# Layer 0 scan of a two-layer MetaFormer: two PSUM buffers for the product, one for the spread B, two for the front's tiles

## The chip, the cores and the metric

The kernel runs on one core of a Trainium2 chip. The time is the device time of that core in microseconds (us), from a few runs of the same program; a profiled execution of its own gives the trace and the profile page.

## What is computed

The input x is 2 images of 96 channels and 96 x 96 pixels. Layer 0 adds a selective-scan mixer and a small feed-forward network, layer 1 an attention mixer and another such network. The change concerns the scan of layer 0, which the reference states so (cut to the scan):

```python
def step(hst, inputs):
    ut, dt, bt, ct = inputs
    dA = jnp.exp(dt[..., None] * A)
    hst = hst * dA + (dt * ut)[..., None] * bt[:, :, None, :]
    y = jnp.einsum('bkdn,bkn->bkd', hst, ct)
    return (hst, y)
...
out_y = selective_scan(xs4, delta, A, Bs, Cs, Ds.reshape(KG, d_inner))
inv_y = out_y[:, 2:4, :, ::-1]
...
y = out_y[:, 0] + inv_y[:, 0] + wh_y + invwh_y
```

There are 192 inner channels, 16 states per channel and 4 directions (along rows and along columns, each forwards and backwards). The recurrence runs over windows of 6 x 6 pixels, each a sequence of 36 steps of its own. What leads to it (a layer norm, a projection, a 3 x 3 convolution, an offset sampling, and the projections to delta, B and C) and what follows (a layer norm, a gate, a projection, the feed-forward network) are the front and the back below.

## The kernel before

**Stripes.** Layer 0 is cut into 32 stripes: 2 images of 16 stripes, each of 6 rows or 576 tokens. For each stripe there is a front (`_l0_front`), a scan (`_l0_scan`) and a back (`_l0_back`). While stripe n is scanned, the front of stripe n + 1 and the back of an earlier stripe run in between on the same engines.

**Units.** The scan of a stripe is 64 units: 2 halves of the channels (h), 4 directions (o for rows or columns, kk for forwards or backwards), 4 groups of states (i) and 2 halves of the tokens (c). A unit holds 32 channels x 4 states on the 128 partitions, and 3 blocks of channels x 288 tokens along the free axis, 864 elements in all. With 32 stripes that makes 2048 units. A unit u is worked through in this order (`unit` in `_l0_section`):

- TensorE (PE) spreads B of the tokens over the partitions, with a matmul against a 0/1 matrix, into the PSUM tile `B` (L1040)
- VectorE (DVE) multiplies it with delta times u, `dur`, into the PSUM tile `bp` (the product, L1045; 864 floats, so two of PSUM's eight banks)
- VectorE scans: h = h x dA + bp along the tokens, into the SBUF tile `h` (L1060). The decays `dA` come from ScalarE (ACT, L1025), three instructions for two units
- GpSimd (POOL) multiplies h with C, `cre`, in place (L1065)
- PE folds the 4 states of a channel into one by matmuls that add into the PSUM tile `y` (L1077). One `y` tile gathers 32 units; it starts with a matmul of the inputs (L966, L968), and ACT copies it out at the end (L976, L978)

SyncE (SP) issues all loads: `dlr`, `dur` and `cre`.

**The front and the back** hold some matmuls for each stripe (72 steps of the convolution among them, L551), copies and activations out of PSUM on ACT, and elementwise work on POOL (L609 to L615, L743 to L746, L921). VectorE has three small kinds of instruction from there: `xn` (L508), `fxq` (L827) and `Y` (L912). The PSUM tiles of the front and back are all called `p`: one bank each, `P.np` of them in turn.

**The order.** Every operation goes into a plan (`_Plan`) with its engine, a cost, a due time and the tiles that it uses. The planner sets them in order engine by engine: what can start first goes first, and of those what is due first; a tile takes a buffer when one is free. The result is a fixed order on each engine, which the program keeps. At run time each instruction waits, by semaphores, for what it depends on, and an engine stands still behind an instruction that waits. A change in the number of buffers thus changes both the waits and the whole order.

**PSUM in layer 0** before the change: `B` two banks (two buffers), `bp` two banks (one buffer), `y` one, `p` three: all eight. `h` has six buffers (`P.nh`), `dA` two (`P.nda`).

**The hand-set waits.** Besides the dependencies that follow from the tiles, `product` of an even unit (c = 0) is made to wait for what the scan of this unit and of the next will need: the decays of unit u, B of unit u + 1, and the POOL and PE instructions that free the h buffer of unit u + 1. `wait` does this with the list of `P.issued`.

Of the kernel before, what the change touches and what calls it, by code (L numbers as in the profile page):

```python
# [55 lines left out]
def _in_order(k, tc, start, engines=ENGINES):  # L56

    last = {}
    for i in k.nc.cur_bb.bb.instructions[start:]:
        if i.engine in engines:  # L60
            if i.engine in last:
                tc.add_manual_dep(
                    i,
                    last[i.engine].name,
                    mybir.DependencyInfo(
                        mybir.DependencyClass.NoSync, mybir.DependencyReason.DATA
                    ),
                    reason="in_order",
                )
            last[i.engine] = i  # L70
# [915 lines left out]
def _tail(py, b):  # L986

    n = T - HEAD
    return py.ap[NBL * CB :, b * n : b * n + n]


def _l0_section(k, P, S, f, first, o, h, kk, py, at, tau):


    nc = k.nc
    latest = lambda: nc.cur_bb.bb.instructions[-1]

    def wait(keys):
        for other in map(P.issued.get, keys):
            if other is not None:  # L1000
                P.tc.add_manual_dep(
                    latest(), other.name,
                    mybir.DependencyInfo(mybir.DependencyClass.Sync, mybir.DependencyReason.DATA),
                    reason="with_the_product")

    kg = o + 2 * kk
    reps = []
    for name, d in (("dlr", f.dl[kg]), ("dur", f.du[kg])):
        t = S.tile(P.rep, [128, NBL, T], name, 2)
        S.op("sp", 2.6, lambda t=t, d=d: nc.sync.dma_start(  # L1010
            t.ap.rearrange("p b t -> p (b t)"),
            d.ap[:, 3 * h : 3 * h + 3, :].rearrange("c b t -> c (b t)").unsqueeze(1)
            .to_broadcast([CB, NQ, NBL * T])), (d,), (t,), due=at - 9 * tau)
        reps.append(t)
    dlr, dur = reps

    def quarter(i):
        t0, u = at + 2 * i * tau, first + 16 * o + 8 * kk + 2 * i
        cre, dA = S.tile(P.rep, [128, T], "cre", 4), S.tile(P.rep, [128, 2, NBL, H2], "dA", P.nda)
        S.op("sp", 1.0, lambda: nc.sync.dma_start(  # L1020
            cre.ap, f.cd[o].ap[kk, :, i, :].unsqueeze(0).to_broadcast([CB, NQ, T])),
            (f.cd[o],), (cre,), due=t0 - P.early["sp"] * tau)
        for blk in range(NBL):
            def decay(blk=blk):
                nc.scalar.activation(  # L1025
                    dA.ap[:, :, blk, :], dlr.ap[:, blk, :].rearrange("p (c n) -> p c n", c=2),
                    AF.Exp, scale=k.A[:, i, kg, h, blk : blk + 1])
                P.issued["act", u] = latest()

            S.op("act", 0.76, decay, (dlr,), ((dA, blk),), due=t0 - P.early["act"] * tau, tab="e")  # L1030
        for c in range(2):
            unit(u + c, i, c, cre, dA, t0 + c * tau)

    def unit(u, i, c, cre, dA, t0):
        toks = slice(c * H2, (c + 1) * H2)
        pB, bp = S.tile(P.ps, [128, 512], "B", 2), S.tile(P.ps, [128, 1024], "bp", 1)
        ht = S.tile(P.rep, [128, NBL, H2], "h", P.nh)

        def spread():
            nc.tensor.matmul(  # L1040
                pB.ap[:, :H2], k.selb[:, kk, i, :], f.bc[o].ap[:, toks], start=True, stop=True)
            P.issued["B", u] = latest()

        def product():
            nc.vector.tensor_tensor(  # L1045
                bp.ap[:, : NBL * H2].rearrange("p (b n) -> p b n", b=NBL), dur.ap[:, :, toks],
                pB.ap[:, :H2].unsqueeze(1).to_broadcast([128, NBL, H2]), ALU.mult)
            if c == 0:
                free = u + 1 - P.nh
                wait([("act", u), ("B", u + 1), ("pool", free), ("pe", free)])  # L1050

        S.op("pe", 0.3, spread, (f.bc[o],), (pB,), due=t0 - P.early["pe"] * tau)
        S.op("dve", 1.13, product, (dur, pB), (bp,), due=t0 - P.early["dve"] * tau)

        def scan():
            hv, dv = (v.rearrange("p b n -> p (b n)") for v in (ht.ap, dA.ap[:, c]))
            bv = bp.ap[:, : NBL * H2]
            if kk:
                hv, dv, bv = hv[:, ::-1], dv[:, ::-1], bv[:, ::-1]
            nc.vector.tensor_tensor_scan(hv, dv, bv, 0.0, ALU.mult, ALU.add)  # L1060

        S.op("dve", 2.0, scan, (dA, bp), (ht,), due=t0 + (1.35 - P.early["dve"]) * tau)

        def times_c():
            nc.gpsimd.tensor_tensor(  # L1065
                ht.ap, ht.ap, cre.ap[:, toks].unsqueeze(1).to_broadcast([128, NBL, H2]), ALU.mult)
            P.issued["pool", u] = latest()

        S.op("pool", 2.06, times_c, (cre,), (ht,), due=t0 + (2.3 - P.early["pool"]) * tau)

        def states():
            end = o == 1 and kk == 1 and i == NQ - 1

            def part(dst, v, stop):
                if o:
                    v = v.rearrange("p (w j i) -> p w i j", i=WIN, j=WIN)
                nc.tensor.matmul(dst, k.fold, v, start=False, stop=stop)  # L1077

            for blk in range(NBL):
                dst = py.ap[CB * blk : CB * blk + CB]  # L1080
                n = HEAD - H2 if c else H2
                part(dst[:, c * H2 : c * H2 + n], ht.ap[:, blk, :n], end and c == 1)
            if c:
                for blk in range(NBL):
                    part(_tail(py, blk), ht.ap[:, blk, n:], end and blk == NBL - 1)
            P.issued["pe", u] = latest()

        S.op("pe", 1.0, states, (ht,), (py,), due=t0 + (3.5 - P.early["pe"]) * tau)

    for i in range(NQ):  # L1090
        quarter(i)


def _layer0(k, tc, a, x, x2d):


    nc = k.nc
    with ExitStack() as st:
        P = Ctx()
        pool = lambda name, bufs, **kw: st.enter_context(tc.tile_pool(name=name, bufs=bufs, **kw))  # L1100
        cp = pool("l0c", 1)
        P.dram = pool("scr", 1, space=DRAM)
        with ExitStack() as ws:
            tmp = ws.enter_context(tc.tile_pool(name="l0t", bufs=1))
            wps = ws.enter_context(tc.tile_pool(name="l0p", bufs=1, space=PSUM))
            _l0_weights(k, a, cp, tmp, wps, P.dram)
            ffn = _ffn_weights(k, cp, tmp, "f0", a["W1_0"], a["b1_0"], a["W2_0"], a["b2_0"])
        P.rep, P.hand, P.back, P.front = (pool(n, 1) for n in ("rep", "hand", "back", "front"))
        P.ps = pool("ps0", 1, space=PSUM)
        P.tc, P.issued = tc, {}  # L1110
        P.early = {"pe": 60, "act": 60, "dve": -30, "pool": 0, "sp": 8}
        P.np, P.ng, P.nda, P.nh = 3, 5, 2, 6
        start = len(nc.cur_bb.bb.instructions)
        S, tau = _Plan(k), 3.4
        stripes = [(b, s) for b in range(NB) for s in range(NW)]
        F = [Ctx() for _ in stripes]

        def front(n):
            if n < len(stripes):
                t0, t1 = (64 * n - 90) * tau, (64 * n - 12) * tau  # L1120
                _l0_front(k, P, S, F[n], x, *stripes[n], lambda v: t0 + v * (t1 - t0))

        def back(n):
            b, s = stripes[n]
            t0, t1 = (64 * n + 68) * tau, (64 * n + 135) * tau
            _l0_back(k, P, S, F[n], ffn, x[b, :, s * WIN : (s + 1) * WIN, :],
                     x2d[b, :, s * T : (s + 1) * T], lambda v: t0 + v * (t1 - t0))

        front(0)
        for t, name in zip(k.kvq, ("k_w", "v_w", "q_w")):  # L1130

            S.op("sp", 0.2, lambda t=t, name=name: nc.sync.dma_start(t, a[name]), due=64 * tau)
        for n in range(len(stripes)):
            front(n + 1)
            _l0_scan(k, P, S, n, F[n], tau)
            back(n)
        S.issue()
        _in_order(k, tc, start, ENGINES + (mybir.EngineType.SP,))
# [709 lines left out]
def tile_metaformer(ctx: ExitStack, tc: tile.TileContext, a, out):  # L1848
# [34 lines left out]
    scratch = ctx.enter_context(tc.tile_pool(name="x2d", bufs=1, space=DRAM))  # L1883
    x2d = scratch.tile([NB, C, NTOK], F32, tag="x2d", name="x2d")
    _layer0(k, tc, a, a["x"], x2d)
    _layer1(k, tc, a, x2d, out)

# [61 lines left out]
```

## Time and profile before

| | |
|---|---|
| median of 3 runs | 8775.34 us (8774.3 to 8780.41) |
| span of the profiled execution | 8782.9 us |
| busy over the span: VectorE (DVE) | 8004.4 us, 91% |
| TensorE matmuls (PE) | 7366.0 us, 84% |
| ScalarE (ACT) | 6381.2 us, 73% |
| GpSimd (POOL) | 6026.5 us, 69% |
| first and last product (L1045) start at | 146.8 and 6727.2 us |
| mean granted TensorE clock | 0.891 of full speed |

For the profiled execution only the span is known; its run time is not listed apart. The page gives busy shares over the whole span, but layer 1 begins after 6735 us and has other limits, so shares for the change have to be read over the stretch of layer 0. In a row of groups, the first number is the sum of the busy time, the second the mean of one instruction; after the second bar stands the idle time of the engine just before such instructions, and what ended most of it. Start times and durations in a timeline are rounded to 0.01 us. A gap is a start minus the end of the instruction before it on the engine; a negative gap means that the two records overlap.

### The profile page before, as it was taken

How to read it: one execution, taken by the hardware profiler on the slowest of the kernel's cores; microseconds unless marked ns; L12 is line 12 of the kernel's file. 1: busy time of each engine (PE TensorE's matmuls, PEld its weight loads, DVE VectorE, ACT ScalarE, POOL GpSimd, SP SyncE). 2: the span in 40 equal slices, each digit the busy share in tenths (PEclk: the TensorE clock that was granted, in tenths of full speed). 3: DMA queues.
4: the chain of work that ended last, by engine and by line, in shares of the span. 5: the costliest groups of instructions: out<-in, count | busy, mean ns of one | idle time of the engine just before them, and what ended most of it. 6: DMA issues, size and time to landing. Idle time of an engine off the chain costs nothing. (4 is left out here: it accounts for less than half of the span.)

```text
span 8782.9 us, 119686 instructions
## 1 busy us (share of the span) xinstructions
PE 7366.0 (84%) x43653; PEld 3436.2 (39%) x43653; DVE 8004.4 (91%) x5398; ACT 6381.2 (73%) x10720; POOL 6026.5 (69%) x3835
## 2 busy tenths in 40 slices
PE   7888888888888888888888888888865999989998
PEld 4333434434434343343343434334422323542245
DVE  3899999999999999999999999999997898959988
ACT  5677777777777777777777777777764787678867
POOL 4999998988899899898998888898885000010001
PEclk8898888998988888898888889888866999989999
DMA  2444444444444444444444444444442000110001
GB/s 85 139 149 144 145 145 141 146 143 141 142 141 145 137 151 144 142 142 146 145 142 143 142 143 138 145 139 142 142 140 87 19 2 9 34 51 2 3 21 32
DMA packets 339996, 985.64 MB, mean 112 GB/s; under 512 B 50152, under 2 KB 51872, under 8 KB 339104
## 3 DMA queue, kind: packets, MB, share of 16 engines
q1 hardware_dynamic: 337488, 977.74, 35.4%
q8 instruction: 346, 5.67, 0.3%
q14 instruction: 258, 2.11, 0.1%
q10 hardware_dynamic: 1904, 0.12, 0.0%
HBM read 797.19 MB, written 139.25 MB: 107 GB/s over the span
## 5 line engine op out<-in xcount | busy, mean ns | idle before, releaser
L1065 POOL TENSOR_TENSOR h<-h,cre 128x864 f32<-128x864 f32 x2048 | 4124.1, 2023 | 692.6 <-DVE h L1060 493.1
L1060 DVE TENSOR_TENSOR_SCAN h<-dA,bp 128x864 f32<-128x864 f32 x2048 | 3999.8, 1953 | 84.7 <-PE y L1077 6.3
L1025 ACT ACTIVATE dA<-dlr,A 128x576 f32<-128x576 f32 x3072 | 2156.4, 765 | 1098.8 <-DVE h L1060 1015.1
L1045 DVE TENSOR_TENSOR bp<-dur,B 128x864 f32<-128x864 f32 x2048 | 2172.9, 1061 | 295.9 <-PE B L1040 48.7
L1077 PE MATMUL y<-h,fold 128*32 128x288 f32 (+2 forms) x18432 | 1870.7, 452 | 161.6 <-POOL h L1065 152.0
L1040 PE MATMUL B<-bt,selb 128*128 128x288 bf16 x2048 | 642.4, 315 | 963.5 <-DVE bp L1045 951.1
L551 PE MATMUL pc<-xin,off 96*96 96x288 f32 x4608 | 1321.4, 414 | 0.5 <-ACT xin L516 0.4
L1077 PEld LDWEIGHTS y<-h,fold 128*32 128x32 f32 x18432 | 764.3, 119 | 1138.1 <-issue 548.9
L1413 ACT ACTIVATE pr<-sc 128x960 f32<-128x960 f32 (+1 forms) x1080 | 954.1, 937 | 200.3 <-PE sc L1409 180.3
L1493 DVE TENSOR_TENSOR sums<-sums,pr 128x3840 f32<-128x3840 f32 (+1 forms) x240 | 959.1, 3996 | 55.2 <-ACT pr L1413 33.2
L551 PEld LDWEIGHTS pc<-xin,off 96*96 96x96 f32 x4608 | 708.3, 165 | 514.3 <-issue 268.4
L1585 POOL MEMSET vch<- 96x32 f32 x16 | 2.4, 153 | 1296.6 <-DVE dist L1447 1209.3
L1040 PEld LDWEIGHTS <-selb 128*128 128x128 bf16 x2048 | 200.6, 99 | 1303.7 <-DVE bp L1045 797.9
L1409 PE MATMUL sc<-qH,kH 32*128 32x480 f32 (+1 forms) x3240 | 627.2, 602 | 9.7 <-issue 4.9
L1409 PE MATMUL sc<-q,kH 32*128 32x480 f32 (+1 forms) x1080 | 564.5, 602 | 0.0
L1475 PE MATMUL av<-pr,vT 128*32 128x480 f32 (+1 forms) x4320 | 532.6, 564 | 3.7 <-ACT av L1500 3.5
L1666 DVE SCALAR_TENSOR_TENSOR acc<-vch,lepe_w,acc 96x1152 f32<-96x1152 f32 x320 | 469.2, 1466 | 7.9
L867 POOL TENSOR_TENSOR x<-x,fy 96x576 f32<-96x576 f32 x32 | 56.1, 1755 | 480.6 <-ACT fy L866 400.6
L1409 PEld LDWEIGHTS sc<-qH,kH 32*128 32x128 f32 x3240 | 219.2, 184 | 418.3 <-issue 218.4
L724 PE MATMUL pt<-xd,w_dt 96*128 96x288 f32 x768 | 313.4, 500 | 26.4 <-ACT zs L534 14.8
L743 POOL TENSOR_TENSOR e<-e,du 128x576 f32<-128x576 f32 x192 | 271.6, 1414 | 31.5 <-ACT du L739 31.3
L745 POOL TENSOR_TENSOR dl<-dl,r 128x576 f32<-128x576 f32 x192 | 270.8, 1410 | 6.2
(270 smaller groups left out, 10159.0 us busy)
## 6 DMA issues: line engine op xcount, KB each, us to landing
cre<-c_d SPq DMA_DIRECT2D x1024, 288.0 KB
dur<-du_d SPq DMA_DIRECT2D x256, 864.0 KB
dlr<-dl_d SPq DMA_DIRECT2D x256, 864.0 KB
x<-xs SPq DMA_DIRECT2D x512, 72.0 KB
du_d<-du SPq DMA_DIRECT2D x128, 288.0 KB
dl_d<-dl SPq DMA_DIRECT2D x128, 288.0 KB
du_d<-du SPq DMA_DIRECT2D x128, 144.0 KB
dl_d<-dl SPq DMA_DIRECT2D x128, 144.0 KB
```

Of the source, the lines that this page charges most:

```text
L551: pe(H2, lambda: nc.tensor.matmul(pc.ap[:C, :H2], k.w_c1[:, ih, tap, oh * C : (oh + 1) * C], xin.ap[:, ih, 3 * c + dy : 3 * c + dy + 3, dx ...
L1025: nc.scalar.activation(dA.ap[:, :, blk, :], dlr.ap[:, blk, :].rearrange("p (c n) -> p c n", c=2), AF.Exp, scale=k.A[:, i, kg, h, blk : blk ...
L1040: nc.tensor.matmul(pB.ap[:, :H2], k.selb[:, kk, i, :], f.bc[o].ap[:, toks], start=True, stop=True)
L1045: nc.vector.tensor_tensor(bp.ap[:, : NBL * H2].rearrange("p (b n) -> p b n", b=NBL), dur.ap[:, :, toks], pB.ap[:, :H2].unsqueeze(1).to_bro ...
L1060: nc.vector.tensor_tensor_scan(hv, dv, bv, 0.0, ALU.mult, ALU.add)
L1065: nc.gpsimd.tensor_tensor(ht.ap, ht.ap, cre.ap[:, toks].unsqueeze(1).to_broadcast([128, NBL, H2]), ALU.mult)
L1077: nc.tensor.matmul(dst, k.fold, v, start=False, stop=stop)
L1409: nc.tensor.matmul(two[to // 2][:, to % 2, :n], kH[rows, k0 : k0 + 128], q, start=True, stop=True)
L1413: nc.scalar.activation(pr[:, 2 * i : 2 * i + 2, :n], two[i][:, :, :n], AF.Exp, scale=HD**-0.5)
L1475: nc.tensor.matmul((main if s < HEADS else other)[s * HD : (s + 1) * HD, :n], vT[:, blk, hd, :], pr[:, place(s, p), :n], start=at == 0, st ...
L1493: nc.vector.tensor_tensor(both, both, pr[:, :, :, :n], ALU.add)
L1666: S.op("dve", 1.43, lambda: nc.vector.scalar_tensor_tensor(acc.ap, src(), W.lw[:, t : t + 1], acc.ap, ALU.mult, ALU.add), (vch,), (acc,))
```

## The change

The product gets a second buffer in PSUM (two more banks). They are taken from `B`, which goes from two buffers to one, and from the tiles `p`, which go from three to two. Since B of unit u + 1 can no longer be made before product u has read B of unit u, that entry leaves the hand-set waits of product u: it would wait for itself.

```diff
     def unit(u, i, c, cre, dA, t0):
         toks = slice(c * H2, (c + 1) * H2)
-        pB, bp = S.tile(P.ps, [128, 512], "B", 2), S.tile(P.ps, [128, 1024], "bp", 1)
+        pB, bp = S.tile(P.ps, [128, 512], "B", 1), S.tile(P.ps, [128, 1024], "bp", 2)
         ht = S.tile(P.rep, [128, NBL, H2], "h", P.nh)
...
             if c == 0:
                 free = u + 1 - P.nh
-                wait([("act", u), ("B", u + 1), ("pool", free), ("pe", free)])
+                wait([("act", u), ("pool", free), ("pe", free)])
...
         P.early = {"pe": 60, "act": 60, "dve": -30, "pool": 0, "sp": 8}
-        P.np, P.ng, P.nda, P.nh = 3, 5, 2, 6
+        P.np, P.ng, P.nda, P.nh = 2, 5, 2, 6
```

The planner lays out all of layer 0 anew: the order of product and scan on VectorE stays alternating, while the instructions of the front and back stand at other places between them on every engine.

## The prediction

> **What bounds the kernel now.** I read the page's busy shares first, then its groups of instructions, then the busy table over windows, the waits of VectorE and TensorE, and last the timeline of VectorE. All that the change touches lies in layer 0, whose products run from 146.8 to 6727.2 us; layer 1 after that stays as it is.
>
> The page, groups of instructions (line, engine, tile, shape, count | busy us, mean ns | idle before, what ended it):
>
> ```profile
> L1065 POOL TENSOR_TENSOR h<-h,cre 128x864 f32<-128x864 f32 x2048 | 4124.1, 2023 | 692.6 <-DVE h L1060 493.1
> L1060 DVE TENSOR_TENSOR_SCAN h<-dA,bp 128x864 f32<-128x864 f32 x2048 | 3999.8, 1953 | 84.7 <-PE y L1077 6.3
> L1045 DVE TENSOR_TENSOR bp<-dur,B 128x864 f32<-128x864 f32 x2048 | 2172.9, 1061 | 295.9 <-PE B L1040 48.7
> ```
>
> One busy row of the middle (PE, PEld, DVE, ACT, POOL):
>
> ```profile
> 3000.00:4000.00 1000.00, 822.72 (x4825) 402.63 (x4822) 950.97 (x653) 741.74 (x1282) 899.61 (x557) 0.89 0.45 142
> ```
>
> VectorE (DVE) is the bound: 95% busy, and only two instructions per unit fill it, the product L1045 and the scan L1060. POOL follows at 90%, PE at 82%. A stripe (64 units) takes 6580.4 / 2047 x 64 = 205.7 us. Where is VectorE's idle time? VectorE's waits, here over 300 to 6600 us, name little of it; TensorE's show that B is early (waiter <- releaser: us in total, times, longest):
>
> ```profile
> DVE bp L1045 <- PE B L1040: 44.6, 48, 2.6
> PE B L1040 <- DVE bp L1045: 884.1, 965, 2.9
> PE y L1077 <- POOL h L1065: 118.7, 171, 1.8
> ```
>
> The timeline of VectorE shows the rest, in gaps too short to be listed as waits:
>
> ```profile
> 4000.90 0.42 DVE L827 TENSOR_TENSOR fxq<-fxc,fva 96x288 fp8e5<-96x288 f32 x1
> 4001.25 1.05 DVE L1045 TENSOR_TENSOR bp<-dur,B 128x864 f32<-128x864 f32 x1
> 4002.33 1.96 DVE L1060 TENSOR_TENSOR_SCAN h<-dA,bp 128x864 f32<-128x864 f32 x1
> 4004.32 1.06 DVE L1045 TENSOR_TENSOR bp<-dur,B 128x864 f32<-128x864 f32 x1
> ...
> 4011.78 1.95 DVE L1060 TENSOR_TENSOR_SCAN h<-dA,bp 128x864 f32<-128x864 f32 x1
> 4013.87 1.06 DVE L1045 TENSOR_TENSOR bp<-dur,B 128x864 f32<-128x864 f32 x1
> ```
>
> The scan of 4002.33 ends at 4004.29 and the next product starts 0.03 us later; after the scan of 4011.78 it is 0.14 us. But fxq (L827), which waits for nothing on its own engine, overlaps its successor: it ends at 4001.32 and the product had started at 4001.25. I sorted all 1918 direct scan-to-product steps of layer 0 by the waits that the program puts on the product. 903 with only a VectorE wait (the scan that read the one bp buffer): median 0.04 us. 713 with PE, VectorE, ACT and POOL: 0.14. 252 with a DMA besides: 0.23. 46 with PE and VectorE: 0.11. Of some 320 steps into or out of xn, fxq and Y (L508, L827, L912), nearly all are -0.07 to -0.09, the products with four waits behind them too.
>
> **What the Trainium skill says.** "Perfetto Trace Analysis", section "DVE / Act Engine Instruction": the end that the profiler reports includes the acknowledgement of the writes, and the next instruction may begin before it. The trace agrees (-0.08 us without a wait, +0.03 with one). "VectorE: DVE Perf Modes", section "The DRAIN you can't avoid", says that a semaphore between VectorE instructions costs nothing extra; here it costs 0.11 us, and the measurement decides. "Perfetto Trace Analysis", section "Identifying Dependency Chains": an instruction that waits for several engines may get separate wait instructions in front. That fits 0.04, 0.14 and 0.23. Section "Optimization Strategy" there: a gap that repeats on the engine that should be saturated can mean too few buffers. That is this gap.
>
> **Part 1, bp with two buffers: the gain.** In the new program the product waits for PE, and on even units for ACT, POOL and at times a DMA, never for VectorE: the scan that read its buffer is two back. All its waits can be over while the scan before it runs, so the step should fall to -0.08 us as behind fxq. The scan still waits for its product (0.035 us), unchanged. All steps sum to 255.7 us now and to 1918 x -0.08 = -153.4 us then: 409 us. Of the 255.7, 57 us are real waits (what is above the class medians: 51 in the four-wait class, 6 in the DMA class); I let them stand. **Gain 352 us**, 11.0 us per stripe. Floor of a unit: 1.953 - 0.08 + 1.061 + 0.035 = 2.97 us, against 3.08 to 3.28 now.
>
> **Part 2, B with one bank: the cost.** B(u+1) may start only after product u. The chain from there is 0.05 us to the start, 0.28 matmul, some 0.06 to VectorE; it fits under the scan (1.95 us) with 1.5 us to spare, if PE is free. Behind the waiting B stand on PE the states y (L1077) of earlier units and the front's matmuls; POOL needs no y soon (six h buffers), but ACT and the front do. How early is B now? In 137 units of 2200 to 2640 us, B ended 4.85 us before its product in the median; 92 of them by 4.7 or more. One bank costs each about a unit, 3.05 us. 129 of 137 then still come in time; the other 8 are short by 9.9 us together, 4.6 us per stripe.
>
> Second look, by POOL. In the new order y(u) stands in front of B(u+3) in 1843 of 2048 units (before: in front of B(u+4) or later). Product start to scan end 3.05, POOL 0.1 + 2.02, y 0.7, B 0.35: 6.2 us, against 3 x 2.97 = 8.9: POOL may be 2.7 us late. POOL's load per unit is 1.99 for h, plus 1.37 for each front instruction put before it. A unit with one front instruction adds 0.4 us of lateness, with two 1.8, with none it takes 1.0 back. Summed along the new POOL order of a middle stripe, lateness passes 2.7 us in two clusters (near units 7 to 11 and 24 to 28), with 4.6 us to pay. Both looks see overlapping stalls, so I take **4.6 us per stripe, 147 us**, not twice that.
>
> **Part 3, tiles p with two buffers.** The front and back have one evacuation less ahead of ACT. In the new order 647 of ACT's releases to PE stand three units after the scan that frees the decays dA ahead of them on ACT (before: none under four). Scan end to B(u+3): 0.1, three dA 2.15, ACT instructions of 0.45 each, PE 1.6, B 0.36, against 5.9: up to two fit, three are even, four or more (34 cases) are late by 0.4 us or so. That is 15 us; table loads (1.28 us) falling in between may make it 100. I take 30. The front before the first product and the back after the last have two p too, with no scan to hide it: estimate under 5 us, taken as nothing. DMAs are the same in number and bytes; SP's order moves with the plan, and cre is fetched 8 planned units ahead. Nothing else is added; ACT has some 45 more table loads, 60 us in its 26% of idle time, which cover them while dA is early (ACT waited 938.5 us for the scan).
>
> **Sum.** 352 - 147 - 30 = 175 us. The profiled execution spans 8782.9 us and would fall to 8608; the median of the runs is 7.6 us lower, 8775.34: **8600 us**.
>
> **The rivals.**
> A, likeliest: as summed. With costs between 70 and 270 us, 8495 to 8695.
> B, everything hides: B and POOL never late, and even the 57 us of real waits shrink. 8775 - 352 = 8423, down to 8400; to 8495 with few stalls. For it: PE waited for products in half of the units. Against it: POOL is busy 183 us per stripe (5852 us in the layer), which against a floor of 64 x 2.97 + 3 = 193 leaves little to catch up with.
> C, slower: B is late as a rule. With one bank, every wait that PE meets between two Bs (for POOL's h, or for ACT behind dA with only two p) reaches VectorE after 1.5 us instead of 4.6. It decides from 352 / 2048 = 0.17 us of lateness per unit, 11 us per stripe. For it: 837 of the 2048 stretches between two Bs hold over 3.0 us of PE work if a conv step (two matmuls) is priced at 0.54 us and a y at 1.0. Against it: conv matmuls follow each other every 0.27 us, y takes 0.57 at full clock, so a stretch of four conv steps and one y is 2.9 us. At 0.25 us per unit, 512 us are lost: 8935.
> D, the gain isn't there: the wait for PE costs what that for VectorE did, so that steps stay at 0.1 us. Then 8775 + 50 to 150. Against it: the products behind fxq.
>
> **How the numbers follow.** A 0.63, B 0.13, C 0.16, D 0.08. A's own range 8495 to 8695, with a tail to 8790. The measurement of this kernel can tell about 0.2%, 18 us, from no change. Faster: B and most of A and a little of C and D: 0.74. Within 0.2%: 0.06. Slower: 0.20. Range 8440 to 8820.
>
> **What would show it.** Part 1 right: scan-to-product steps at -0.08 us in most units, products and scans with unchanged durations; the stretch of products falls to about 6405 us. Part 2 right: VectorE's wait for B grows from 45 us to 100 or 250, in clusters behind y that waits for POOL. C right: that row at 400 us or more, and PE's wait for products small because PE is late. Part 3: VectorE's waits for B that go back to ACT. I would be wrong if a wait for another engine, met early, still held the product back, or if PE's work between Bs were the limit.

## The result and the profile after

| | before | after |
|---|---|---|
| median | 8776.67 us (4 runs) | 8931.98 us (4 runs, 8925.9 to 8939.6) |
| ratio | | 1.0178, 95% interval 1.0164 to 1.0193: slower by 1.8% |
| span of the profiled execution | 8782.9 us | 8935.6 us |
| first to last product | 146.8 to 6727.2 us | 149.7 to 6874.6 us |
| mean granted TensorE clock | 0.891 | 0.872 |

The forecast was 8600 us, with a range up to 8820. The change costs 155 us. In the profiled executions the span grew by 153 us, 145 of them between the first and the last product. Rival C came true, with almost the time that it had been given (8935).

The page of after, its groups of instructions for the same three lines:

```profile
L1065 POOL TENSOR_TENSOR h<-h,cre 128x864 f32<-128x864 f32 x2048 | 4130.0, 2020 | 753.1 <-DVE h L1060 235.2
L1060 DVE TENSOR_TENSOR_SCAN h<-dA,bp 128x864 f32<-128x864 f32 x2048 | 4000.0, 1953 | 74.3 <-ACT dA L1025 3.8
L1045 DVE TENSOR_TENSOR bp<-dur,B 128x864 f32<-128x864 f32 x2048 | 2150.5, 1050 | 534.5 <-PE B L1040 501.0
```

Scan, product and POOL's multiplication take as long as before. What grew is the idle time in front of the product, from 295.9 to 534.5 us, and nearly all of it now ends with B. The busy table for the same 1000 us as before (PE, PEld, DVE, ACT, POOL, clock):

```profile
3000.00:4000.00 1000.00, 838.74 (x4753) 405.51 (x4753) 914.61 (x642) 728.37 (x1244) 874.33 (x542) 0.87 0.44 139
```

VectorE fell from 951 to 915 us and POOL from 900 to 874: no engine is at its limit. TensorE is at its work for longer, 839 us instead of 823, at a lower clock. The waits of after over 300 to 6600 us:

```profile
PE y L1077 <- POOL h L1065: 637.9, 635, 3.0
DVE bp L1045 <- PE B L1040: 484.4, 616, 3.4
PE B L1040 <- DVE bp L1045: 77.5, 161, 1.2
PE pp L932 <- ACT r L730: 60.4, 30, 2.1
```

The order of the rows has turned round. Before, PE waited 884.1 us for VectorE's products and VectorE 44.6 us for B. Now PE waits 77.5 us for products and VectorE 484.4 us for B, and the longest row of PE is its wait for POOL in front of y, 637.9 us instead of 118.7.

Part 1 did what was forecast. VectorE's timeline in a quiet stretch of after:

```profile
4002.49 1.04 DVE L1045 TENSOR_TENSOR bp<-dur,B 128x864 f32<-128x864 f32 x1
4003.56 1.95 DVE L1060 TENSOR_TENSOR_SCAN h<-dA,bp 128x864 f32<-128x864 f32 x1
4005.43 1.04 DVE L1045 TENSOR_TENSOR bp<-dur,B 128x864 f32<-128x864 f32 x1
```

The scan ends at 4005.51 and the next product has begun at 4005.43: -0.08 us. Of 1952 direct scan-to-product steps the median is -0.08 us, and in such a stretch a unit takes 2.94 us. So the loss sits in few places. The lateness of the products (start minus end of the instruction before, above -0.09 us) adds to 19.4 us per stripe, of which units 5, 11, 12, 19, 24 and 26 (counted from 1 in each stripe) hold over 11. One cluster, at units 11 and 12 of a stripe, on three engines, beginning with POOL:

```profile
2283.69 1.40 POOL L612 TENSOR_TENSOR bot<-dif,fr 96x576 f32<-96x576 f32 x1
2285.05 2.01 POOL L1065 TENSOR_TENSOR h<-h,cre 128x864 f32<-128x864 f32 x1
2287.02 1.30 POOL L613 TENSOR_TENSOR bot<-bot,xin 96x576 f32<-96x576 f32 x1
2288.40 1.40 POOL L614 TENSOR_TENSOR bot<-bot,top 96x576 f32<-96x576 f32 x1
2289.76 2.03 POOL L1065 TENSOR_TENSOR h<-h,cre 128x864 f32<-128x864 f32 x1
```

PE over the same time (in brackets the idle time before, and what ended it; `px` are the front's matmuls that add the parts of the offset sampling, L623, and `yc` those of the back's layer norm, L892):

```profile
2287.11 0.95 PE L1077 MATMUL y<-h,fold 128*32 128x216 f32 x12 [2.42 <-POOL h L1065]
...
2291.84 1.18 PE L1077 MATMUL y<-h,fold 128*32 128x288 f32 x6 [1.26 <-POOL h L1065]
2292.95 1.27 PE L623 MATMUL px<-top,ident 96*96 96x288 f32 x2
...
2295.94 1.17 PE L623 MATMUL px<-bot,ident 96*96 96x288 f32 x2
2296.90 0.45 PE L1040 MATMUL B<-bt,selb 128*128 128x288 bf16 x1
```

And VectorE:

```profile
2292.55 1.95 DVE L1060 TENSOR_TENSOR_SCAN h<-dA,bp 128x864 f32<-128x864 f32 x1
2297.48 1.06 DVE L1045 TENSOR_TENSOR bp<-dur,B 128x864 f32<-128x864 f32 x1 [2.97 <-PE B L1040]
```

Read it upwards. VectorE waits 2.97 us for a B of 0.45 us. That B could have started when the product before it had read its bank (about 2292.5), but in front of it on PE stood a y that waited 1.26 us for POOL, and four pairs of px. The y had begun at 2291.84 and was through by 2292.95, so of the 4.4 us by which this B started late, some 0.5 us are that y's and 3.9 the px's. POOL was late because up to two front instructions of 1.3 to 1.4 us stood between its multiplications. The px pairs took 1.17 us here, and 0.65 to 0.73 us in stretches with a full clock.

### The profile page after: what moved, and what is told of

It reads as the page before. It is cut to its first block, busy times and chain, and to the rows that moved or that the text cites. A ratio compares the mean times of both kernels' runs of the same rounds, so it can differ in the third digit from the quotient of the medians.

```text
span 8935.6 us, 118880 instructions
## 1 busy us (share of the span) xinstructions
PE 7609.3 (85%) x43653; PEld 3515.4 (39%) x43653; DVE 7881.7 (88%) x5398; ACT 6444.0 (72%) x10766; POOL 6018.0 (67%) x3835
## 5 line engine op out<-in xcount | busy, mean ns | idle before, releaser
L1065 POOL TENSOR_TENSOR h<-h,cre 128x864 f32<-128x864 f32 x2048 | 4130.0, 2020 | 753.1 <-DVE h L1060 235.2
L1060 DVE TENSOR_TENSOR_SCAN h<-dA,bp 128x864 f32<-128x864 f32 x2048 | 4000.0, 1953 | 74.3 <-ACT dA L1025 3.8
L1045 DVE TENSOR_TENSOR bp<-dur,B 128x864 f32<-128x864 f32 x2048 | 2150.5, 1050 | 534.5 <-PE B L1040 501.0
L1077 PE MATMUL y<-h,fold 128*32 128x288 f32 (+2 forms) x18432 | 1914.7, 459 | 770.8 <-POOL h L1065 721.3
L1040 PE MATMUL B<-bt,selb 128*128 128x288 bf16 x2048 | 664.2, 324 | 125.9 <-DVE bp L1045 123.2
L842 ACT CAST fh<-fph 128x288 f16<-128x288 f32 x384 | 142.4, 393 | 357.0 <-PE fph L839 356.7
L729 ACT ACTIVATE e<-pt,dt_b 128x288 f32<-128x288 f32 x384 | 189.6, 494 | 185.4 <-PE pt L724 173.5
```

What stands on the lines that cost most here:

```text
L1040: nc.tensor.matmul(pB.ap[:, :H2], k.selb[:, kk, i, :], f.bc[o].ap[:, toks], start=True, stop=True)
L1045: nc.vector.tensor_tensor(bp.ap[:, : NBL * H2].rearrange("p (b n) -> p b n", b=NBL), dur.ap[:, :, toks], pB.ap[:, :H2].unsqueeze(1).to_bro ...
L1065: nc.gpsimd.tensor_tensor(ht.ap, ht.ap, cre.ap[:, toks].unsqueeze(1).to_broadcast([128, NBL, H2]), ALU.mult)
```

## The experiments

Differences below are against the runs of before that were made beside each kernel (medians from 8773 to 8783 us).

### The new order with all buffers of before

The planner of the changed kernel makes its order; `B` then gets two banks, `bp` one buffer, `p` three. (`where` holds the free buffer that each p takes.)

```diff
+REAL = {"B": 2, "bp": 1, "p": 3}
...
                     n = [s is t.slot for s in t.slots].index(True)
+                    if t.tag == "p" and id(t) in self.where:
+                        n = self.where[id(t)]
+                    elif t.tag in ("B", "bp"):
+                        seen[t.tag] = seen.get(t.tag, -1) + 1
+                        n = seen[t.tag] % REAL[t.tag]
```

> The changed kernel's order with all buffers of before: B two banks, bp one, p three. It splits the 224 us by which this order with two tiles p lost (9000 us). If the loss is the order's: 8970 to 9010 us. If it is the waits for one of two tiles p that make it: 8776 to 8850 us, and TensorE's waits for ScalarE's instructions that free a p go.

Measured: 8972.36 us, ratio 1.0227 (1.021 to 1.0245). The new order, with no buffer changed, costs 199 us. Not all of that is order: the entry for B is missing from the hand-set waits here too, so the products of odd units wait for PE besides VectorE, and their median step behind a scan is 0.10 us, against 0.04 before. That is an estimated 40 to 60 us of the 199 (0.07 us for each of at most 964 steps, less where longer waits hide it). Its waits over 300 to 6600 us:

```profile
PE y L1153 <- POOL h L1141: 876.5, 848, 3.2
DVE bp L1121 <- PE B L1116: 132.6, 167, 3.3
```

y is the first row again. With two banks, B ended 4.85 us before its product in the old order (median of the units of 2200 to 2640 us; this is B's lead below), and 1.81 us in this one. The planner laid out this order for one bank, and y(u) stands in front of B(u+3) in it; a second bank at run time cannot move B forward.

### The new order with one buffer less at a time

The same edit with other numbers: `{"B": 2, "bp": 1}` with two tiles p, then `{"B": 1, "bp": 1}`.

> The changed kernel's order of instructions on every engine (two products stand behind the scan instead of ahead of it), but with two banks for B, in turn, and one buffer for bp. Bank theory (B is late because one bank lets PE run only one unit ahead): VectorE's wait for B falls from 487 us to under 100 us. The product then waits for VectorE again and, on odd units, for PE besides (0.11 us by the class of 46 before, against 0.04), so 8776 + 1024 x 0.07 = 8850 us, 8820 to 8880. Order theory (the planner's new order, made for two tiles p, is what makes B late): the wait for B stays at 300 to 500 us and the time is above 9050 us.

> The changed kernel's order with one bank for B and one buffer for bp: the fourth corner to the two orders with one and two banks. If bp's second buffer is worth its 352 us in the new order too: 9250 to 9300 us, more than the 9174 us that order (+224) and bank (+174) make when added to 8776. If the two add up without more, 9150 to 9200 us, and bp's second buffer is worth only some 240 us here.

Measured: 8999.78 us (1.0246, 1.0229 to 1.0263), and 9023.13 us (1.0279, 1.0262 to 1.0296). The first lies between its two theories, the second is under both of its own. Put in a row, as differences to before:

| order | B | bp | p | us above before |
|---|---|---|---|---|
| new | 2 | 1 | 3 | 199 |
| new | 2 | 1 | 2 | 219 |
| new | 1 | 1 | 2 | 248 |
| new (the change) | 1 | 2 | 2 | 155 |

Each of these is uncertain by some 15 us, so a difference of two by some 20. Two tiles p cost 20 us, the bank of B 29 (both hardly clear of that), and the second bp gives back 92: not the 352 of the sum. The shares hold for this sequence of steps; the second bp was measured only as the last one, behind a B that had lost its lead. Where the other 260 went shows in VectorE's lateness before products, by what ended it:

| us | short gaps and VectorE itself | PE's B | others | sum |
|---|---|---|---|---|
| before | 328 | 53 | 95 | 477 |
| new order, buffers of before | 374 | 157 | 101 | 633 |
| new order, one B, one bp, two p | 375 | 195 | 98 | 668 |
| the change | 27 | 560 | 31 | 618 |

The second bp takes 348 us of short gaps away, and 365 us of waits for B come in. VectorE reaches the same late B sooner and stands there longer.

### One part alone, and one bank in the old order

The old plan with `B` moved right behind the product before it and one bank (first), and the planner's own orders for `B` one (second) and `p` two (third). With one bank the entry for B leaves the hand-set waits; all else is as before.

```diff
-        pB, bp = S.tile(P.ps, [128, 512], "B", 2), S.tile(P.ps, [128, 1024], "bp", 1)
+        pB, bp = S.tile(P.ps, [128, 512], "B", 1), S.tile(P.ps, [128, 1024], "bp", 1)
```

```diff
-        P.np, P.ng, P.nda, P.nh = 3, 5, 2, 6
+        P.np, P.ng, P.nda, P.nh = 2, 5, 2, 6
```

> The order of the kernel before on every engine, bp one buffer and p three as there, but B with one bank: B of unit u + 1 stands right behind product u in the program, which on PE moves it by less than a unit; nothing else moves. This prices the prediction's part 2 by itself (4.6 us per stripe, 147 us, read from how early B was in this very order). If that price was right, VectorE's wait for B rises from 45 to 120 to 230 us; the product of odd units now waits for PE too (0.11 us for 0.04, 72 us), so 8781 + 72 + 75 to 185 = 8930 to 9040 us. If the price was wrong for any order (lockstep multiplies it, the clock drops), the wait for B is 350 us or more and the time 9150 us or more.

> The kernel before with B at one bank and the planner's own new order for it (bp one, p three). Order theory (the planner, which prices VectorE's reply to PE at 1.5 us, lays y and the front's work closer in front of B): wait for B 250 us or more, above 9050 us. Bank theory: as before_order_one_b, within 60 us.

> The kernel before with two tiles p instead of three and the planner's own order for it. If two tiles p do harm by themselves (PE waits for ACT's copies and its clock drops), 1% or more: above 8870 us. If B's lead of 4.85 us covers them, within 0.6%, 8730 to 8830 us.

Measured: 8950.15 us (1.0196, 1.0179 to 1.0213), 8983.77 (1.0233, 1.0216 to 1.025) and 9153.56 (1.0426, 1.0409 to 1.0443). In the old order the bank costs 168 us beside the 147 of the sum, and B's lead fell to 1.76 us, as 4.85 less 3.05 had said. But it came otherwise than the sum had it. The products of odd units wait for PE here as well (median step 0.10 us instead of 0.04 over 949 steps), an estimated 60 us that have nothing to do with a late B. And of the waits, most are put down to y, on PE like B:

```profile
DVE bp L1066 <- PE y L1098: 85.2, 64, 4.1
DVE bp L1066 <- PE B L1061: 35.4, 47, 1.6
```

The planner's own order for one bank costs hardly more than the old one with B moved: 8984 against 8950 us, the side of the bank theory. For p two, VectorE's wait for B is 44 us, as before, but its scans wait for h buffers that y frees late:

```profile
DVE h L1060 <- PE y L1077: 277.2, 57, 15.5
```

The same two tiles cost 20 us in one order and 372 in another that the planner made.

### The old order with all new buffers

The old plan; one B right behind the product, two bp, and two p, with work that wants a third p put off, and what depends on it.

```diff
+REAL = {"B": 1, "bp": 2, "p": 2}
...
-        for o in self.order():
+        for o in self.two(self.first(self.order())):
```

> The kernel before with its own plan, and all of the change's buffers given to it afterwards: B one bank (its spread right behind the product before it), bp two, p two (the work that wants a third p put off until one is free). Theory, the new order is the failing step and the prediction's sum holds for the old one: 8776 less 352 for bp, plus the 174 us that one bank cost in the old order, plus 30 for p: 8600 to 8680 us. Rival, one bank and two tiles p cost as much in any order: 8880 to 8980 us.

Measured: 8975.79 us, ratio 1.0221 (1.0204 to 1.0238): the rival's side. The new order is then not the only bad one, and the sum does not hold for this one either, though its scan-to-product steps are at -0.08 us too (median). The putting off makes an order of its own, with single waits for B of up to 9.2 us, so the run does not price the buffers in an untouched order; that could not be had with two tiles p.

### y behind the next B

Each y group is held back in the new order until the next B has been passed, unless something needs it.

```diff
+            if o.kind == "y":
+                held.append(o)
+                continue
...
+            if o.kind == "B":
+                out += held
+                held = []
```

> The changed kernel with one thing moved: on PE each group of y matmuls stands behind the next B instead of in front of it, where no other instruction between them depends on it. Buffers, and the order on all other engines, stay. POOL theory (B stands behind y, and y waits for POOL's h): the late units 5, 11, 12, 14 and half of 19 and 20 of each stripe go, 7 to 9 us of the 19.4 us per stripe, so 8932 - 225 to 290 = 8640 to 8710 us. Work theory (PE has too much work of its own between two Bs): the same work only shifts by a unit, and 8900 to 8950 us remain.

Measured: 8776.28 us, ratio 0.9995 (0.9987 to 1.0004). That is 160 us less than the change, some 60% of what the theory asked for. Its waits:

```profile
DVE bp L1063 <- PE B L1058: 371.3, 324, 3.8
PE y L1095 <- POOL h L1083: 183.1, 190, 2.3
```

PE's wait for POOL fell from 638 to 183 us, and lateness from 19.4 to 14.1 us per stripe. So y in front of B was a cause, shown by its removal: unit 26 lost its 1.4 us per stripe, unit 5 went from 2.4 to 1.1. What is left sits at units 11 and 19. Unit 11, the first of the cluster above, was not relieved (2.4 us before the move, 3.1 after it), as its timeline suggests: there px held B up for longer than y.

> As the run with y behind the next B (8776 us), and the px matmuls, which wait for GpSimd, behind the next B as well. If px in front of B is what keeps units 11 and 12 late (3.3 and 0.9 us of each stripe's 14.1), some 3 us per stripe go: 8680 to 8720 us, and unit 11 is no longer the latest. If it is TensorE's clock or its amount of work there, 8760 to 8790 us.

Here px was held back like y. Measured: 8765.35 us, ratio 0.9988 (0.9982 to 0.9995). At the late unit px had not moved. PE's timeline in this run:

```profile
2242.60 1.18 PE L1096 MATMUL y<-h,fold 128*32 128x288 f32 x6 [1.57 <-POOL h L1084]
2243.71 1.27 PE L641 MATMUL px<-top,ident 96*96 96x288 f32 x2
...
2247.65 0.45 PE L1059 MATMUL B<-bt,selb 128*128 128x288 bf16 x1
```

The rule lets a px go as soon as work that reads it is next in the plan, and that came before the B. The question about px at units 10 to 12 stays open.

> The changed kernel with B of unit u + 1 right behind product u in the program, so that PE takes it ahead of all that the planner put in the 1.6 us between. If B is late because of what stands in front of it within that stretch (y that waits for POOL, px, parts of the convolution), VectorE's wait for B falls from 487 to under 300 us, more than y_behind_b won (371): 8650 to 8740 us. If PE pays for it by waiting for products in front of B, and its clock drops further, 8780 us or more.

Here B was put right behind the product before it in the program's order. Measured: 8882.17 us, ratio 1.0114 (1.0097 to 1.0131); VectorE's waits for B are still 388 us, and PE waits 440 us for products in front of B (77.5 in the change). That is the second case of the expectation in its time and in PE's waits, but not in the clock, which did not drop (0.876, against 0.872).

### pp in five operations

The five pairs that make `pp` (4.9 us together at half clock) become operations of their own, so that a B can go between. (`pp` is the back's output projection, L932.)

```diff
-        op("pe", 5 * H2, run, (Y, zs, (x1, c)), (pp,))
+        for n, (w, v) in enumerate(parts):
+            op("pe", H2, lambda n=n, w=w, v=v: nc.tensor.matmul(
+                pp.ap[:C, :H2], w, v(), start=(n == 0), stop=(n == 4)),
+               (Y, zs, (x1, c)), (pp,))
```

> The changed kernel with the back's output projection pp (5 steps, two passes each, one operation for the planner, 5 us on PE) handed to the planner as five operations, so that B can go in between. Work theory: the lateness of units 19, 20, 24 and 26 (2.8, 0.7, 0.8, 1.5 us per stripe) goes for the most part, 4 to 5.5 us per stripe: 8755 to 8805 us. POOL theory: units 19 and 26 are late because y in front of B waits for POOL's h, and at most 1 us per stripe is won: 8900 to 8930 us.

> The changed kernel with both edits tried before: y behind the next B (155 us won alone) and pp as five operations (65 us alone). If the two gains are of separate stretches of PE, they add: 8932 - 220 = 8712 us, 8690 to 8740; if y_behind_b's remaining lateness at unit 19 (3.5 us per stripe, 112 us) is all pp at half clock, 8650 to 8690 us.

Measured: 8866.78 us (1.0097, 1.008 to 1.0114) alone, which is 70 us less than the change and between the two theories; and 8770.64 us (0.9987, 0.998 to 0.9995) with y behind B, only 7 us less than y behind B alone, and above both expected ranges. A new plan puts the late units elsewhere (20 instead of 19), and the gains do not add up.

### The clock

TensorE's clock stood at 0.50 in the clusters. The Trainium skill, "TensorE: Matmul & The Clock Gate", Part 1, has half clock as the state of an engine that was idle of late. The trace agrees with the two levels (2296 us of the change at 0.50, the rest at 1.00). It agrees less with the reason: PE was busy for 14.24 of the 15.50 us of the last window below, and stayed at 0.50. Is the clock the cause, or does it follow from the waits? Matmuls with a zero weight, added to y, fill stretches between two B; in all these runs they stand ahead of the y of their unit.

```diff
+            for _ in range(S.fill):
+                nc.tensor.matmul(
+                    py.ap[:CB, :H2], k.nil, k.selb.rearrange("p k i n -> p (k i n)")[:, :H2],
+                    start=False, stop=False)
```

> The changed kernel, its order kept, with up to 8 filler matmuls (zero weights of 32 columns, 288 columns of a constant, so that they add 0 to y) on PE ahead of a y, only where the plan puts less than 2.3 us of other work between two Bs: 6424 in all, some 0.12 us each. They run while PE would wait for POOL. Clock theory (PE's waits let its clock fall to half, its next work takes twice as long, and with one bank that makes B late; of 454 us of large lateness from 1000 to 6000 us 306 fall in stretches at a clock of 0.6 or less): the mean clock rises from 0.872 to above 0.90, VectorE's wait for B falls by 150 to 300 us, to 8650 to 8790 us. Waits theory (the releases by POOL and ACT themselves are late, the clock is only a symptom): the wait for B stays within 60 us of 487, or grows by the fillers' own time, 8930 to 9050 us.

> Control: the same fillers in the kernel before. There B is 4.85 us early in the median and VectorE waits for it 45 us in all; both theories expect the time within 0.4% of 8781 us, the clock theory a higher mean clock than 0.891.

> The changed kernel with five matmuls by a zero weight behind each y of all stretches between two B that hold less than two convolution steps (some 7300 in the layer), so that TensorE idles less just where the clusters of late products are (units 5, 11, 12, 19). Theory 1, the lateness of the clusters is TensorE at half clock: about half of the 560 us of lateness goes, less some 60 us for the filler: at most 8800 us. Theory 2, the lateness is the waits of y and px for GpSimd and ScalarE themselves, and the clock only follows from them: 8900 us or more, with units 11 and 19 still the latest.

Measured: 8905.5 us (1.0123, 1.0106 to 1.014) with 6424 matmuls where little work stood, which left the clusters as they were; 8760.38 us (0.9975, 0.9965 to 0.9985) for before with the same rule; 8917.51 us (1.0154, 1.0137 to 1.0171) with 7300 in all stretches with less than two convolution steps. The first lies between its two theories, and VectorE's wait for B did not fall (522 us in the profiled execution). Its six runs spread from 8884 to 8966 us, the two longest with the lowest mean clock (0.931, the others 0.939 to 0.946), so its median is less certain than the rest. The last one reached the cluster of the profile above. Its windows (last three columns: clock, DMA share, GB/s):

```profile
2277.00:2288.50 11.50, 9.55 (x68) 5.11 (x63) 9.33 (x8) 5.68 (x13) 11.42 (x8) 1.00 0.48 149
2288.50:2304.00 15.50, 13.46 (x100) 7.58 (x101) 12.89 (x10) 8.49 (x18) 15.01 (x11) 1.00 0.48 142
```

In the change itself the later window had this:

```profile
2288.50:2304.00 15.50, 14.24 (x52) 6.28 (x54) 9.01 (x8) 7.96 (x16) 12.64 (x8) 0.50 0.50 151
```

Of the lateness above 0.25 us between 1000 and 6000 us, 309 of 453 us lay at a clock of 0.6 or less in the change (mean over the 2 us before the product), and 79 of 439 here. Yet the time fell by only 15 us, which is within the noise, lateness stays at 608 us against 618, and units 11 and 19 are still the latest, as theory 2 had said. So filler that brings the full clock does not mend the clusters. The filler takes PE time of its own in front of B (0.79 us for five), so the run sets no price on the clock itself; what a full clock without filler would do is not shown.

### A version that beats both

y behind the next B, pp in five operations and the first filler rule together; then the same with px behind B and the second rule.

> The two edits and the fillers together. Clock theory: what remains of the lateness after the two edits (some 300 us) halves again: 8500 to 8600 us. Waits theory: no gain over the two edits, 8690 to 8760 us.

> All edits together: y and px behind the next B, pp in five operations, filler in stretches with less than two convolution steps. The version without px behind B and with less filler took 8688.5 us. If both causes (order and clock) add up: 8600 to 8660 us; if filler in the dense stretches costs what it brings: 8680 to 8720 us.

Measured: 8688.51 us, ratio 0.9892 (0.9875 to 0.9908), so 1.1% faster than before and 2.8% faster than the change (0.9892 / 1.0178); and 8753.12 us (0.9968, 0.9955 to 0.998). Here the filler was worth 82 us (8770.64 without it), with the mean clock at 0.966 instead of 0.884: less than the clock theory had asked for, but no longer nothing. Where y no longer holds B up, the clock counts. The second run loses most of this again; as it differs in two things, px and the rule of the filler, which of them does it is not shown.

### The product without PSUM

The product is written into `h` and scanned in place; B gets three banks, p four.

```diff
-        S.op("dve", 1.13, product, (dur, pB), (bp,), due=t0 - P.early["dve"] * tau)
+        S.op("dve", 1.13, product, (dur, pB), (ht,), due=t0 - P.early["dve"] * tau)
```

> The product is written into the SBUF tile h and the scan works on it in place, so that bp needs no PSUM; B then has three banks and p four, and the planner puts the next product ahead of the scan, so that neither step waits for the instruction just before it. If products and scans keep their durations (1.05 and 1.95 us) and all steps fall to -0.08 us, VectorE needs 2.86 us per unit, and POOL with 5852 us busy in the layer becomes the bound: 8280 to 8450 us. If the scan or product gets slower with both operands in SBUF beside POOL, by 0.2 us each or more, it is above 8700 us.

Measured: 11506.32 us, ratio 1.311 (1.3089 to 1.3132), mainly for a reason of the hardware that is told below: of the 2725 us that were lost, the busy time of the scans grew by 2085.

## Why the prediction was wrong

**Part 1, the gain of 352 us.** Its mechanism is shown: steps at -0.08 us, and short gaps down from 328 to 27 us. Its worth in time did not come. In the new order the second bp is worth 92 us, because 365 us of waits for B grew in its place. The step "Sum. 352 - 147 - 30" took gains and losses as independent; they lie in series in front of the same instruction.

**Part 2, the cost of B: the failing step.** The prediction gave VectorE 147 us of waiting for B; the waits for B grew by 507 us, from 53 to 560. "One bank costs each about a unit, 3.05 us. 129 of 137 then still come in time" was worked out from the leads of the old order, at the old pace of VectorE. Two things were left out.

The first is the new order, which "Nothing else is added" priced at nothing. It puts B later: the lead is 1.81 us with two banks and 0.66 in the change, where it is under 0.2 us in 53 of the 132 units from 2200 to 2640 us. This order costs 199 us with all buffers of before (40 to 60 of them, as said, through the hand-set waits). The prediction had it in hand: it had counted that y(u) stands in front of B(u+3) in 1843 units.

The second is the pace. VectorE without its short gaps comes sooner to a B that is no earlier, and waits for B go from 195 to 560 us. This is the larger part. Order, bank and tiles p together cost 248 us, which the prediction's own range for costs (70 to 270) still holds; it is the 260 us of gain that did not come that make the kernel slower.

For the old order the price of one bank looks right (168 us measured, 147 said), but in part by luck: an estimated 60 of the 168 are the extra waits of the odd products. The 9.9 us behind the 147 come to some 7 when each unit's own distance to the product before it is taken from the trace. Nor is the old order a cure, since it loses 200 us with all new buffers. The seven kernels, the change among them, that differ from before in these buffers and the order they bring, and whose lead is 0.66 to 1.81 us, lost 155 to 248 us, whether the order or the bank took the lead away.

**The look at POOL** saw the right place and the wrong size. It allowed POOL to be 2.7 us late and expected two clusters with 4.6 us to pay. There are five or so, with over 11 us per stripe. The cluster above shows two things that it left out: y is not followed by B alone but by px or yc, and these run at half clock. What each of them is worth is open.

**Part 3, 30 us.** 20 us were measured in the new order, uncertain by as much: the size fits, while the mechanism (B late behind ScalarE and dA) was not tested by itself. The 372 us for p two alone belong to another order.

**The rivals.** C is what happened, in its place (PE's waits between two B, above all for POOL's h), in its sign (row at 484 us, PE's wait for products 77.5) and in its size: waits for B grew by 507 us, or 15.8 us per stripe, beyond the 11 from which it decides. That the time came within 4 us of its 8935 is in part luck, since the 0.25 us per unit behind it was an example and not worked out. Its other leg, stretches with four convolution steps, was minor: some 3 us per stripe at units 52 to 60. A chance of 0.16 was too little, because its best evidence, the new order, was used only for POOL and not for B's lead. D did not happen. B's floor was not reached.

**What stays open:** how much of the clusters px holds by itself, the price of the clock in them, and what the second bp would be worth behind a B that keeps its lead.

## What to carry to other kernels

When a planner lays out the work anew, price the change in the new order: take each operation's new neighbours on its queue and the durations of the old trace, and ask how early each operand is there. A gap removed on the busiest engine is worth only what the next wait in front of the same instruction leaves of it. And operations that wait for a slow engine belong behind the one that the bound engine needs next; moving y behind B was worth 160 us here, as much as the whole change cost.

## What the runs showed of the hardware

- A scan with both operands in SBUF ran slower beside POOL. The page of the run without PSUM:

```profile
L1064 POOL TENSOR_TENSOR h<-h,cre 128x864 f32<-128x864 f32 x2048 | 5747.8, 2824 | 513.5 <-DVE h L1059 450.3
L1059 DVE TENSOR_TENSOR_SCAN h<-dA,h 128x864 f32<-128x864 f32 x2048 | 6084.3, 2973 | 4.6
```

The scan rose from 1953 to 2973 ns and POOL's multiplication from 2020 to 2824 ns. The Trainium skill, "SBUF — State Buffer", section "Who interferes with whom", says that a VectorE instruction with two SBUF inputs contends with a GpSimd instruction that reads SBUF; the trace agrees: the 289 multiplications of POOL that met no scan in this run took 2013 ns in the mean, and the two scans that met almost no work of POOL 1947 ns, so neither is slow by itself. The product, with one operand in SBUF, kept its speed beside POOL (1029 ns, 1061 before). The two PSUM banks of a `bp` buy the scan's speed.

- In the cluster TensorE's clock fell to 0.50 though no single wait there was longer than 2.42 us; px went from 0.65 to 1.17 us a pair. It is no exception: in 197 of the 202 falls to 0.50 between 150 and 6700 us of the change, no wait of PE in the 6.9 us before was longer than 2.5 us. Filler raised the mean clock of before from 0.891 to 0.948, for 0.25%.
